# A post-norm attention and MoE kernel: three groups of routed sequences instead of seven, experts' rows cleared by an AND, the results' zeros written behind the attention, and more closing steps per matmul step

## The chip, the cores and the metric

The kernel runs on one core of one Trainium2 chip. The metric is the device time of one execution in microseconds. Before the change the median of three runs is 878.83 us (878.65 to 879.22). The profile shows one further execution of its own.

## What is computed

Input `x` has 16 sequences of 512 tokens with 128 features, all float32. Two layers follow, each with a residual and a LayerNorm behind it (post-norm). Cut to what matters here:

```python
# layer 1: linear attention, 16 heads of 8, causal, no softmax
q, k, v = silu(x @ Wq), silu(x @ Wk), x @ Wv          # q and k turned by cos/sin of position
out = ((q @ k.T) * mask) @ v @ Wo * sigmoid(x @ G1 @ G2)
x = layernorm(x + layernorm(out) * gamma + beta)
# layer 2: shared MLP plus a routed one, 8 experts, top 2, capacity 1280
logits = (x * rsqrt(mean(x * x) + eps)) @ router_w.T
topk_p, topk_i = top_k(softmax(logits), 2)            # weights: topk_p / sum(topk_p)
dispatch = argsort(~sel, stable=True)[:, :capacity]    # the first 1280 tokens of each expert
routed = scatter_add(w * valid * (silu(xg @ rg) * (xg @ ru)) @ rd)
shared = (silu(x @ sg) * (x @ su)) @ sd
x = layernorm(x + shared + routed)
```

Of an expert's 1280 places only the first `count` are taken by tokens; the others must add nothing.

## The kernel before

The attention goes by chunks of 128 tokens, 64 of them (`NT`), four to a sequence. The main loop (L799) runs over chunk times `t` and writes out by hand, engine by engine, what TensorE, ScalarE, VectorE and GpSimd do; only the order of SyncE's transfers is left to the framework, which issues them in one queue. In step `t` the loop projects chunk t + 2 (`project`, L419: the matmul at L423 is the first of its step), transposes chunk t + 1 (`turn_over`), makes the energies of chunk t (L506, masked on VectorE at L513) and the values of chunk t - 1 (L539, L548), and updates the running state (`remember`).

Into these steps four other streams are woven.

- `after(b)` (L557) is a generator of some fourteen stages. It finishes a sequence once its four chunks are done: output projection (L563), gate, two LayerNorms, the transposed copy `x1T`, and the router's logits. `advance` takes it on.
- `shared_steps` (L122) is the shared MLP, cut into 24 steps for a sequence: eight gate steps (L134, silu at L136), eight up steps (L147, multiply at L148 into `h`), and eight half down steps (L157, L162). They stand in one list, `feed`, 384 in all. `shared(t)` takes one when its sequence is ready; the loop calls it twice a chunk.
- `route(b0, b1)` (L628) is a generator that routes the tokens of a group of sequences: softmax (Exp at L654, which needs another ScalarE table than Silu and Tanh), the two best experts, then the rank of each token in its expert from two matmuls (L700, L701) and a scan, with `count` carried from group to group. It is 31 VectorE instructions over [128, n, 8] elements, n being the chunks of the group. `sprinkle` takes a few of its stages after each part of a step. `groups` (L191) has seven entries: 4, 4, 2, 2, 2, 1 and 1 sequences.
- When a group is routed, its scatters (two for each chunk, 128 in all) go into `scatters`. `scatter_behind` (L746) sends one: an indirect DMA from GpSimd (L733) that writes 128 rows of `x1` to their places in `xg_dram`. A small GpSimd instruction on `beat` ahead of it paces it to the compute. A row has 132 floats: 128 features, the token's number, the first expert and two weights.

Behind the last chunk a second loop (L847, the tail) goes on with one MLP step at a time, until `turns`, `todo` and `scatters` are empty and twelve further steps (`over`) have passed. One scatter goes out in two steps.

Two DRAM tensors need contents before they are used. `y_dram` (2 x 8192 rows) takes the experts' results and must be zero where no result comes. `xg_dram` holds the experts' rows, and a place that no token takes must read as zeros with the token number `NOBODY`, so that its result goes out of bounds and is dropped. `fill` (L410) writes both in steps 1 to 16 of the main loop: eight DMAs of 1 MB from the tile `zero` (L412), then eight of 660 KB from the tile `empty` (L414). ScalarE makes both tiles (`nought`, L278).

The second part runs the experts. `load_expert` (L879) fetches weights and rows; `turn_rows` (L892) transposes the rows in three parts of 512, 512 and 256 (L899, L900); `targets_of` (L902) works out targets and weights. For each part there are four gate and up matmuls (L1008, L1010; silu at L1012, multiply at L1013). `backs` holds the down projections (L922), each ending in an indirect DMA to `y_dram` (L928). The list `aside` makes the next expert's transposes during the second part of this one.

The final phase (L1034) takes what `feed` still has, one step at a time. Every second step it calls `add_up` (L947), which adds one of the two y rows of a sequence (L955); on every step, once the y rows are there (`landed`), it calls `an_end` (L1025), which takes one stage of `finish_lot` (L963): statistics of one tile (L102, L104), the reciprocal root (pow on GpSimd at L110; after the last silu a Sqrt on ScalarE at L116 and L118), and the scaled copy `res` (L981). A lot is four tiles, but the last four tiles are lots of one. When `feed` is empty the loop goes on with these stages alone.

Of the kernel before, what the change touches and what calls it, by code (L numbers as in the profile page):

```python
# [27 lines left out]
R = D + 4  # L28
NOBODY = 1.0e6
LN_EPS = 1e-5  # L30
# [16 lines left out]
def tile_kernel(  # L47
# [45 lines left out]
    logits = keep.tile([P, NT, E], F32, name="logits")  # L93
    idx = keep.tile([P, 2, NT], I32, name="idx")
    sg_sb = keep.tile([P, IS], F32, name="sg_sb")
    su_sb = keep.tile([P, IS], F32, name="su_sb")
# [93 lines left out]

    groups = [(0, 4), (4, 8), (8, 10), (10, 12), (12, 14), (14, 15), (15, 16)]  # L191
    with ExitStack() as ph:
# [21 lines left out]
        with tc.manual_schedule(engines=ORDERED):  # L214
# [68 lines left out]
            th_sb = cst.tile([P, D + HALF], F32, name="th_sb")  # L283
            nc.scalar.copy(th_sb, pth)
# [12 lines left out]
            cst_tok = cst.tile([P, NC, 2, 16, 2, 8], F32, name="cst_tok")  # L297
            zero = hp.tile([P, 4 * N], F32, tag="h", name="zero")
            empty = hp.tile([P, NS, R], F32, tag="h", name="empty")
            scratch = hp.tile([P, 10, D + HALF], F32, tag="h", name="scratch")  # L300
            turns_of = cst.tile([P, D + HALF], F32, name="turns_of")
            nc.vector.tensor_scalar(turns_of, pth, 1.0 / (2.0 * math.pi), None, ALU.mult)
# [31 lines left out]
        with tc.manual_schedule(engines=ORDERED):  # L334
            angles(0, pth)
            sines(0)
            angles(1, th_sb)
            same(0)

            causal = cst.tile([P, 3, HALF], F32, name="causal")
            nc.gpsimd.tensor_tensor(causal[:, 0, 0:1], scratch[:, 0, 0:1], zcol, ALU.mult)
            nc.gpsimd.memset(causal, 1.0)
            bmask = cst.tile([P, 64], F32, name="bmask")
            nc.gpsimd.memset(bmask, 1.0)
            nc.gpsimd.affine_select(
                bmask, bmask, pattern=[[-16, 8], [0, 8]], compare_op=ALU.is_ge, fill=0.0, base=0, channel_multiplier=1
            )
# [12 lines left out]
            count = cst.tile([P, E], F32, name="count")  # L362
# [4 lines left out]
            toki = cst.tile([P, NT], I32, name="toki")  # L367

        def constants_of_routing():
# [11 lines left out]
            nc.gpsimd.iota(toki, pattern=[[P, NT]], base=0, channel_multiplier=1)  # L381
            nc.vector.tensor_copy(x1[:, :, D], toki)

        def beginning(t):
# [10 lines left out]
        def beginning_done(t):  # L395
            if t == 0:

                nought(zero, 4 * N)
            elif t == 1:

                nought(empty.rearrange("p r d -> p (r d)"), NS * R)
                nc.gpsimd.memset(empty[:, :, D], NOBODY)
            elif t == 2:
                constants_of_routing()


# [221 lines left out]
        def route(b0, b1):  # L628
# [4 lines left out]
            def wide(name):  # L633
                return rp.tile([P, n, E], F32, tag=name, name=f"{name}_{b0}")
# [68 lines left out]
            nc.scalar.copy(tots[:, :, 1:], pin[:, 1].rearrange("p t e -> p e t"))  # L703
            inside = wide("inside")
            nc.scalar.copy(inside, pin[:, 0])
# [7 lines left out]
            yield  # L713
            rank = wide("rank")
            nc.vector.tensor_tensor(rank, sums[:, :, :n].rearrange("p e t -> p t e"), inside, ALU.add)
# [82 lines left out]
        with tc.manual_schedule(engines=ORDERED):  # L798
            for t in range(-2, NT + 1):  # L799
# [46 lines left out]
            t, over, waited = NT + 1, 12, 0  # L846
            while turns or todo or scatters or over:  # L847
                if not (turns or todo or scatters):
                    over -= 1
# [11 lines left out]
                if t % 2 == 0:  # L861
                    scatter_behind(latest[0])
                t += 1


    with ExitStack() as ph:
# [22 lines left out]

        xgTs, targets = {}, {}  # L890

# [10 lines left out]
        def targets_of(e):  # L902
# [89 lines left out]
        with tc.manual_schedule(engines=ORDERED):  # L992
            load_expert(0)
            load_expert(1)
            for o0, n in parts:
                turn_rows(0, o0, n)
            targets_of(0)
            backs = []
            for e in range(E):
                rg_sb, ru_sb, rd_sb, _ = got[e]  # L1000
                for o0, n in parts:
                    aside = []
                    if o0 == parts[1][0] and e + 1 < E:
                        aside = [lambda q=q: turn_rows(e + 1, *q) for q in parts] + [lambda: targets_of(e + 1)]
                    h = ep.tile([P, IR // P, N], F32, tag="eh", name=f"eh_{e}_{o0}")
# [28 lines left out]
            while feed or ends:  # L1034
# [62 lines left out]
```

## Time and profile before

| What | Value |
|---|---|
| median of the runs | 878.83 us |
| the profiled execution: time, span | 876.59 us, 874.7 us |
| granted TensorE clock, mean | 0.987 |
| ScalarE table loads | 16 of 1.283 us, 7 of them at L654 and as many behind those |
| MLP steps in the attention loop, in the tail, in the final phase (by the program's order) | 102, 124, 158 |
| scatters still to send when the attention ends | 56 of 128 |
| y_dram fills | 8 of 1024 KB, issued from 20.2 to 42.7 us |
| xg_dram fills | 8 of 660 KB, issued from 43.2 to 55.8 us |
| scatters | 128, 1039 ns of GpSimd each, from 181.6 to 494.6 us |
| experts' rows: first load issued, landed | 498.13, 502.62 us |
| last TensorE instruction ends | 860.8 us |

How to read it: an engine's busy time is the time in which one of its instructions ran; a matmul's end is modelled, so TensorE can be busy and still be slowed. A row of a timeline gives start, length, engine, line, operation, written and read tiles, how many alike were merged, and in brackets the idle time of the engine before it with what ended it; "issue" there means that nothing recorded was waited for. Float32 matmuls appear twice, as two passes. One view lists the busy time of each engine in chosen stretches of the span.

### The profile page before, as it was taken

What the parts mean: (1) busy time and instruction counts of PE and PEld (TensorE: products, weight loads), DVE (VectorE), ACT (ScalarE), POOL (GpSimd) and SP (SyncE); (2) the same over time, 40 slices, a digit from 0 to 9 for tenths busy, and PEclk for the clock granted to TensorE, in tenths of its full rate; (3) what the DMA queues carried; (4) which work ended last, traced back from release to release, by engine and by line L of the source; (5) the groups of instructions that cost most, each with busy time, mean ns of one, the idle gap of its engine ahead of it and who ended that gap; (6) DMA issues with size and microseconds to landing.
All of it is one profiled execution on the core that took longest, in us unless ns stands there. A gap on an engine that the chain in (4) does not pass through costs nothing. (4 is left out here: it accounts for less than half of the span.)

```text
span 874.7 us, 24501 instructions
## 1 busy us (share of the span) xinstructions
PE 826.3 (94%) x9792; PEld 567.3 (65%) x9792; DVE 554.1 (63%) x1705; ACT 449.4 (51%) x1302; POOL 334.2 (38%) x443
## 2 busy tenths in 40 slices
PE   6789999999989999999999999999999999999993
PEld 4566667667855765766666657777676776666663
DVE  7588888998888888978533343333333324785454
ACT  7677777577776767564322223333333332433434
POOL 2122222156655556486766413433333431001100
PEclk9899999999999999999999999999999999999997
DMA  7881111011111110000000233322132003650011
GB/s 215 323 343 34 32 34 33 30 36 58 58 40 52 57 52 27 22 29 16 11 6 1 87 88 92 95 80 65 60 92 64 25 25 112 178 169 25 25 37 48
DMA packets 64340, 62.87 MB, mean 72 GB/s; under 512 B 6180, under 2 KB 55132, under 8 KB 63202
## 3 DMA queue, kind: packets, MB, share of 16 engines
q1 hardware_dynamic: 57426, 50.35, 18.4%
q0 software_dynamic: 6656, 10.69, 3.7%
q8 instruction: 77, 1.26, 0.6%
q10 hardware_dynamic: 144, 0.26, 0.1%
q14 instruction: 37, 0.30, 0.1%
HBM read 32.62 MB, written 31.88 MB: 74 GB/s over the span
## 5 line engine op out<-in xcount | busy, mean ns | idle before, releaser
L733 POOL DMA_INDIRECT xg_dram<-x,idx x128 | 133.0, 1039 | 42.1 <-issue 36.7
L136 ACT ACTIVATE sl<-pg 128x512 f32<-128x512 f32 x128 | 76.2, 596 | 125.4 <-PE pg L134 124.6
L1013 DVE TENSOR_TENSOR eh<-esl,peu 128x512 f32<-128x512 f32 (+1 forms) x96 | 57.5, 599 | 127.8 <-PE peu L1010 127.8
L928 POOL DMA_INDIRECT y_dram<-y,to x80 | 77.8, 972 | 154.1 <-ACT y L926 154.1
L148 DVE TENSOR_TENSOR h<-sl,pu 128x512 f32<-128x512 f32 x128 | 87.5, 684 | 77.0 <-PE pu L147 64.6
L134 PE MATMUL pg<-x1T,sg_sb 128*128 128x512 f32 x256 | 131.9, 597 | 1.5 <-ACT sl L136 0.7
L147 PE MATMUL pu<-x1T,su_sb 128*128 128x512 f32 x256 | 131.0, 593 | 1.0 <-ACT sl L136 1.0
L513 DVE TENSOR_TENSOR et<-pe,causal 128x384 f32<-128x384 f32 x256 | 124.4, 547 | 9.6 <-PE pe L506 9.5
L157 PEld LDWEIGHTS pd<-sd_sb,h 128*128 128x128 f32 x1024 | 118.7, 192 | 5.8 <-issue 5.2
L157 PE MATMUL pd<-sd_sb,h 128*128 128x128 f32 x1024 | 121.9, 275 | 0.2 <-DVE add L494 0.2
L110 POOL TENSOR_TENSOR rstd<-ve,neghalf 128x4 f32<-128x4 f32 x44 | 47.2, 1073 | 194.2 <-DVE ve L108 168.0
L922 PEld LDWEIGHTS ped<-rd,eh 128*128 128x128 f32 x640 | 84.0, 192 | 24.6 <-issue 22.7
L1008 PE MATMUL peg<-xgT,rg 128*128 128x512 f32 (+1 forms) x192 | 84.6, 522 | 0.0
L1010 PE MATMUL peu<-xgT,ru 128*128 128x512 f32 (+1 forms) x192 | 84.4, 521 | 0.0
L922 PE MATMUL ped<-rd,eh 128*128 128x128 f32 x640 | 84.3, 275 | 0.0
L1012 ACT ACTIVATE esl<-peg 128x512 f32<-128x512 f32 (+1 forms) x96 | 50.5, 526 | 55.9 <-PE peg L1008 53.9
L147 PEld LDWEIGHTS pu<-x1T,su_sb 128*128 128x128 f32 x256 | 45.7, 190 | 46.0 <-issue 39.9
L926 ACT ACTIVATE y<-ped,wt 128x128 f32<-128x128 f32 x80 | 29.4, 368 | 84.6 <-PE ped L922 84.6
L134 PEld LDWEIGHTS pg<-x1T,sg_sb 128*128 128x128 f32 x256 | 44.3, 191 | 38.4 <-issue 33.7
L506 PE MATMUL pe<-q,kT 32*64 32x192 f32 x2048 | 62.1, 341 | 3.3 <-issue 2.8
L423 PE MATMUL pq<-W,xT 128*128 128x384 f32 x128 | 60.3, 554 | 4.6 <-ACT vlow L444 2.6
L448 DVE TENSOR_TENSOR hat<-qk,cst_tok 128x512 f32<-128x512 f32 x64 | 45.0, 704 | 20.4 <-ACT qk L431 20.3
(178 smaller groups left out, 1260.4 us busy)
## 6 DMA issues: line engine op xcount, KB each, us to landing
y_dram<-zero SPq DMA_DIRECT2D x8, 1024.0 KB, 11.5
y<-y_dram SPq DMA_DIRECT2D x32, 256.0 KB, 3.3
xT<-xt SPq DMA_DIRECT2D x15, 384.0 KB, 3.1
xg_dram<-empty SPq DMA_DIRECT2D x8, 660.0 KB, 9.2
xg<-xg_dram SPq DMA_DIRECT2D x8, 660.0 KB, 4.5
x<-x SPq DMA_DIRECT2D x16, 256.0 KB, 3.5
o<-res SPq DMA_DIRECT2D x15, 256.0 KB, 2.3
xg_dram<-x,idx POOLq DMA_INDIRECT x128, 2.3
```

Source lines behind the costliest of these rows:

```text
L134: nc.tensor.matmul(pg, sg_sb[:, ts(i, P)], seq, start=True, stop=True)
L136: nc.scalar.activation(sl, pg, AF.Silu)
L147: nc.tensor.matmul(pu, su_sb[:, ts(i, P)], seq, start=True, stop=True)
L148: nc.vector.tensor_tensor(h[i // half][:, i % half, :], h.pop(("s", i)), pu, ALU.mult)
L157: nc.tensor.matmul(pd, h[k][:, i - k * half, ts(c, P)], sd_sb[:, i, :], start=(i == 0), stop=(i == IS // P - 1))
L506: nc.tensor.matmul(pes[g][mine, s], kT[rows, s, mine], q2[rows, s, 3 * i : 3 * i + 3], start=(s == 0), stop=(s == 1),)
L513: nc.vector.tensor_tensor(et.rearrange("p s k n -> p s (k n)"), pes[g].rearrange("p s k n -> p s (k n)"), causal.rearrange("p k n -> p (k ...
L733: i = nc.gpsimd.indirect_dma_start(out=xg_dram[:, :], out_offset=bass.IndirectOffsetOnAxis(ap=idx[:, k, t : t + 1], axis=0), in_=x1[:, t, ...
L922: nc.tensor.matmul(pd, h[:, i, ts(c, P)], got[e][2][:, i, :], start=(i == 0), stop=(i == IR // P - 1))
L928: i = nc.gpsimd.indirect_dma_start(out=y_dram[:, :], out_offset=bass.IndirectOffsetOnAxis(ap=to[:, at : at + 1], axis=0), in_=y, in_offset ...
L1008: nc.tensor.matmul(pg[:, :n], rg_sb[:, ts(i, P)], xgTs[e][:, ds(o0, n)], start=True, stop=True)
L1010: nc.tensor.matmul(pu[:, :n], ru_sb[:, ts(i, P)], xgTs[e][:, ds(o0, n)], start=True, stop=True)
```

## The change

Five things are changed.

- `groups` becomes (0, 6), (6, 12), (12, 16). The last one is routed behind the attention.
- `xg_dram` is no longer filled. `clear_rows` makes two masks for each expert from the place's number and `count`: all ones where the place is taken, else 0; and `NOBODY`, now the integer 1 << 20, where it is not. The rows are ANDed with the first as integers, and the targets ORed with the second.
- `y_dram` is zeroed in the tail: sixteen DMAs of 512 KB, one every fourth step, from the first 512 floats of a tile of the attention (`vpads[0][0]`), which ScalarE clears when the attention is over. The tail also waits for `fills`.
- `aside` is kept over the parts of an expert, since it now has seven entries instead of four.
- In the final phase `an_end` is called twice on every odd step, and twice on every step once `feed` is empty.

Some small tiles move: `count` and `slotno` are kept to the end, `th_sb`, `turns_of`, `inside` and `rank` share the space of others.

```diff
-NOBODY = 1.0e6
+NOBODY = 1 << 20
...
-    groups = [(0, 4), (4, 8), (8, 10), (10, 12), (12, 14), (14, 15), (15, 16)]
+    groups = [(0, 6), (6, 12), (12, 16)]
...
+            nc.gpsimd.iota(sloti, pattern=[[P, NS]], base=0, channel_multiplier=1)
+            nc.vector.tensor_copy(slotno, sloti)
...
         def beginning_done(t):
-            if t == 0:
-
-                nought(zero, 4 * N)
-            elif t == 1:
-
-                nought(empty.rearrange("p r d -> p (r d)"), NS * R)
-                nc.gpsimd.memset(empty[:, :, D], NOBODY)
-            elif t == 2:
+            if t == 2:
                 constants_of_routing()
...
-        y_rows = y_dram.rearrange("(p q r) d -> p q (r d)", p=P, r=4 * N // D)
-        x_rows = xg_dram.rearrange("(p q r) d -> p q (r d)", p=P, r=NS)
+        y_rows = y_dram.rearrange("(p q r s) d -> q p r (s d)", p=P, r=2, s=N // D)

         def fill(i):
-            if i < 8:
-                nc.sync.dma_start(y_rows[:, i, :], zero)
-            elif i < 16:
-                nc.sync.dma_start(x_rows[:, i - 8, :], empty.rearrange("p r d -> p (r d)"))
-
+            nc.sync.dma_start(y_rows[i], zero.unsqueeze(1).to_broadcast([P, 2, N]))
+
+        fills = list(range(2 * T * D // (P * 2 * N)))
...
-                if 1 <= t < 17:
-                    fill(t - 1)
...
             t, over, waited = NT + 1, 12, 0
-            while turns or todo or scatters or over:
-                if not (turns or todo or scatters):
+
+            zero = vpads[0][0].rearrange("p a b d -> p (a b d)")[:, 0:N]
+            nought(zero, N)
+            while turns or todo or scatters or fills or over:
+                if not (turns or todo or scatters or fills):
                     over -= 1
...
                     scatter_behind(latest[0])
+                if t % 4 == 1 and fills:
+                    fill(fills.pop(0))
                 t += 1
...
+        def clear_rows(e, o0, n):
+
+            if o0 == 0:
+                taken[e] = ok = ep.tile([P, 2, NS], I32, tag="ok", name=f"ok_{e}")
+                nc.vector.tensor_scalar(ok[:, 0], slotno, count[:, e : e + 1], -1.0, ALU.is_lt, ALU.mult)
+                nc.vector.tensor_scalar(ok[:, 1], slotno, count[:, e : e + 1], float(NOBODY), ALU.is_ge, ALU.mult)
+            here = slice(o0 // P, (o0 + n) // P)
+            rows = got[e][3][:, here, :].bitcast(I32)
+            nc.vector.tensor_tensor(
+                rows, rows, taken[e][:, 0, here].unsqueeze(2).to_broadcast([P, n // P, R]), ALU.bitwise_and
+            )
...
             nc.vector.scalar_tensor_tensor(to, second, float(T), xg[:, :, D], ALU.mult, ALU.add)
+            nc.vector.tensor_tensor(to, to, taken[e][:, 1], ALU.bitwise_or)
...
             for o0, n in parts:
+                clear_rows(0, o0, n)
+            for o0, n in parts:
                 turn_rows(0, o0, n)
             targets_of(0)
-            backs = []
+            backs, aside = [], []
...
                 for o0, n in parts:
-                    aside = []
                     if o0 == parts[1][0] and e + 1 < E:
-                        aside = [lambda q=q: turn_rows(e + 1, *q) for q in parts] + [lambda: targets_of(e + 1)]
+                        for step in (clear_rows, turn_rows):
+                            aside += [lambda q=q, f=step, e=e: f(e + 1, *q) for q in parts]
+                        aside.append(lambda e=e: targets_of(e + 1))
...
                 an_end()
+                if begun % 2 == 1 or not feed:
+                    an_end()
```

By the changed program's order the attention loop has 102 MLP steps as before, the tail 156 and the final phase 126.

More of the change, by code (lines that the diff above doesn't have):

```diff
@@ L94, in tile_kernel @@
     idx = keep.tile([P, 2, NT], I32, name="idx")
+    count = keep.tile([P, E], F32, name="count")
+    slotno = keep.tile([P, NS], F32, name="slotno")
     sg_sb = keep.tile([P, IS], F32, name="sg_sb")
@@ L282, in tile_kernel @@
             nc.tensor.matmul(pth, ones[0:1, :], th_row, start=True, stop=True)
-            th_sb = cst.tile([P, D + HALF], F32, name="th_sb")
+            th_sb = wk1.tile([P, D + HALF], F32, tag="w", name="th_sb")
             nc.scalar.copy(th_sb, pth)
@@ L297, in tile_kernel @@
             cst_tok = cst.tile([P, NC, 2, 16, 2, 8], F32, name="cst_tok")
-            zero = hp.tile([P, 4 * N], F32, tag="h", name="zero")
-            empty = hp.tile([P, NS, R], F32, tag="h", name="empty")
             scratch = hp.tile([P, 10, D + HALF], F32, tag="h", name="scratch")
-            turns_of = cst.tile([P, D + HALF], F32, name="turns_of")
+            turns_of = wk1.tile([P, D + HALF], F32, tag="o", name="turns_of")
             nc.vector.tensor_scalar(turns_of, pth, 1.0 / (2.0 * math.pi), None, ALU.mult)
@@ L361, in tile_kernel @@
             startrow = cst.tile([P, E], F32, name="startrow")
-            count = cst.tile([P, E], F32, name="count")
             goes_on = {}
@@ L367, in tile_kernel @@
             toki = cst.tile([P, NT], I32, name="toki")
+            sloti = cst.tile([P, NS], I32, name="sloti")
         def constants_of_routing():
@@ L703, in route @@
             nc.scalar.copy(tots[:, :, 1:], pin[:, 1].rearrange("p t e -> p e t"))
-            inside = wide("inside")
+            inside = rp.tile([P, n, E], F32, tag="sel", name=f"inside_{b0}")
             nc.scalar.copy(inside, pin[:, 0])
@@ L713, in route @@
             yield
-            rank = wide("rank")
+            rank = rp.tile([P, n, E], F32, tag="prob", name=f"rank_{b0}")
             nc.vector.tensor_tensor(rank, sums[:, :, :n].rearrange("p e t -> p t e"), inside, ALU.add)
@@ L888, in load_expert @@
             got[e] = rg_sb, ru_sb, rd_sb, xg
-        xgTs, targets = {}, {}
+        xgTs, targets, taken = {}, {}, {}
+        def clear_rows(e, o0, n):
[8 more added lines that the diff above has]
+            )
         def turn_rows(e, o0, n):
```

## The prediction, made before the changed kernel was run

> **What bounds the kernel now.** I read the page first, then the busy times by stage, then TensorE's timeline inside the stages that lose time, then what stands behind its last matmul.
>
> ```profile
> span 874.7 us, 24501 instructions
> PE 826.3 (94%) x9792; PEld 567.3 (65%) x9792; DVE 554.1 (63%) x1705; ACT 449.4 (51%) x1302; POOL 334.2 (38%) x443
> ...
> DMA  7881111011111110000000233322132003650011
> ```
>
> TensorE is the bound, so only its idle time and stretched stages can be won. The windows name the stages: start, first chunks, one calm group of four, attention with the shared MLP, tail, experts, final phase, and what follows the last matmul. Columns: busy us (instructions) of PE, PEld, DVE, ACT, POOL, then granted clock, DMA share, GB/s.
>
> ```profile
> 0.00:23.15 23.15, 14.49 (x192) 9.38 (x192) 17.07 (x63) 17.19 (x60) 6.07 (x26) 0.91 0.74 226
> 23.15:66.02 42.87, 34.62 (x868) 26.15 (x869) 29.63 (x87) 29.17 (x107) 8.94 (x19) 0.93 0.84 328
> 66.02:84.93 18.91, 17.44 (x448) 12.94 (x446) 17.88 (x59) 14.48 (x54) 6.05 (x7) 1.00 0.13 39
> 84.93:392.00 307.07, 293.98 (x6014) 208.25 (x6013) 267.26 (x878) 215.56 (x721) 151.73 (x183) 0.99 0.13 40
> 392.00:503.80 111.80, 110.11 (x520) 68.61 (x518) 54.28 (x184) 34.13 (x62) 71.55 (x117) 1.00 0.10 26
> 503.80:729.00 225.20, 223.88 (x1118) 155.90 (x1119) 79.47 (x164) 81.75 (x179) 77.75 (x80) 1.00 0.23 66
> 729.00:860.80 131.80, 131.80 (x639) 86.10 (x637) 81.81 (x239) 50.60 (x103) 12.12 (x12) 1.00 0.31 90
> 860.80:874.70 13.90, 0.00 (x0) 0.00 (x0) 6.73 (x37) 6.56 (x18) 0.00 (x0) 0.68 0.19 57
> ```
>
> PE idles 8.7, 8.3, 1.5, 13.1, 1.7, 1.3, 0 and 13.9 us in them. The second stage is the one with the fills (8.4 MB of zeros and 5.4 MB of empty rows, DMA share 0.84); the last is pure tail. TensorE's timeline in the second:
>
> ```profile
> 35.89 0.29 PE L548 MATMUL pout<-et,vpad 128*32 128x64 f32 x7
> 39.27 0.55 PE L548 MATMUL pout<-et,vpad 128*32 128x64 f32 x25 [3.09 <-issue]
> ```
>
> Seven of 32 alike matmuls run, PE stands 3.09 us waiting for nothing recorded, and the other 25 follow. The same cut is at 30.82 (1.35), 56.04 (2.21) and 63.40 (0.58), with the DMA engines 83 to 100% busy at each. I read it as instructions that come late behind the fills.
>
> **The first fills go (L414 for good, L412 to the tail).** Eight chunks from 23.15 to 66.02 take 42.87 us; the four calm ones after them take 18.91. If all eight cost what the calm ones do, 42.87 - 2 x 18.91 = 5.1 is won. But the first four carry hardly any steps of `after`, and a chunk without them takes 3.4 (45.85 to 49.21, 66.02 to 69.50): 3 x 3.4 + 4.7 + 18.91 = 33.8, or 9.1 won. I take 8.0, near the upper end, because the cuts, and the 0.6 to 0.8 clock behind them, lie in those first four. It includes ACT's 1.30 for `empty`. ACT's 1.90 for `zero` wins nothing: ACT waits for DVE right behind it (sines at 21.16). The added iota and copy for `slotno` are two instructions of 0.2, hidden on POOL and 0.2 on DVE.
>
> Here a rule speaks against me. The Trainium skill (Runtime: NRT & Kernel Launch, Instruction fetch mechanics) says that fetching is hidden, since the sequencer issues more slowly than the buffer fills. By it the cuts are something else and stay: the start would win ACT's 1.30 alone. The row shows cuts only while the fills run (none over 0.3 us without a named releaser later, in six thousand matmuls of attention), so I go by the row.
>
> **Three groups instead of seven.** A step of attention starts with L423. Without routing four chunks take 22.50 us (184.66 to 207.16), by chunk 5.41, 5.31, 6.58, 5.20. With it:
>
> ```profile
> 335.76 0.91 PE L423 MATMUL pq<-W,xT 128*128 128x384 f32 x2
> 341.07 0.91 PE L423 MATMUL pq<-W,xT 128*128 128x384 f32 x2
> 351.25 0.81 PE L423 MATMUL pq<-W,xT 128*128 128x384 f32 x2
> ```
>
> The chunk at 341.07 takes 10.18 instead of 6.58. Summed over the six chunks of each route against the calm ones: (0,4) 38.54 - 34.39 = 4.2; (4,8) 40.87 - 34.39 = 6.5; (8,10) 38.41 - 34.39 = 4.0; (10,12) 6.1, its last chunk estimated from (4,8)'s. Sum 20.8. The cheap two lie beside down steps (L157), the dear two beside up steps, which also load ACT and DVE. By the changed program's order, (0,6) routes in chunks 34 to 39, four of them with up steps, and (6,12) exactly where (10,12) did. So 6.5 and 6.1, plus wider rows: the 31 DVE instructions of a route take 8.5 us for two sequences and 8.8 and 10.3 for four, about 1.1 more per two sequences; 20.8 of stretch against 36.0 of DVE time makes 0.6 of that count: 0.6 for (0,6), 1.2 for (6,12). After: 14.4. Won 6.4 (4.7 if the width counts in full, 10.7 if both get the cheap place).
>
> The table loads are inside this: each route costs two of
>
> ```profile
> 340.36 1.28 ACT L654 ACT_TABLE_LOAD   x1
> ```
>
> and the copy before it ends at 340.35. The Trainium skill (ScalarE: Activation LUTs, What ACT_TABLE_LOAD costs) adds a drain of 1.38 us to each switch. By it four loads fewer would free 10.6 us of ACT; the row has no such idle, so 5.1.
>
> In the tail three routes become one; PE's gaps from them (390.49, 399.46, 400.36, 415.32: 0.96 + 0.27 + 0.42 + 0.69 = 2.3) shrink by two thirds: 1.5 (0 to 2.3).
>
> **The zeros in the tail.** Sixteen DMAs of 512 KB, one in four steps. On SP they stand before the first expert's loads only. 1 MB took 2.44 us between landings in the start, so 1.2 us in every 3.5: a third of the DMA engines, which have a share of 0.10 there. Scatters need 1.38 us of POOL per 1.75. PE runs 520 matmuls in 112 us here against 868 in 43 us, so late instructions should not return. ACT's 512 zeros, about 0.6, fall between silus. Cost 0. The tail itself gets 32 steps longer (124 to 156 by the order, since 72 scatters instead of 56 are left when attention ends), and the final phase loses the same 32 (158 to 126): TensorE does them in either place, 0.
>
> **The AND.** Per expert 528 + 528 + 264 elements on DVE. The nearest row with a broadcast operand is L448, 704 ns for 512; so 0.7 + 0.7 + 0.4 and three small ones, 2.3 us in an expert of 27.2 us in which DVE works about 9.5. Behind each stands one `eh` multiply, with three PSUM buffers in front of PE: 0. Only expert 0 is exposed: its rows landed at 502.62, PE's feed ended at 503.79, and it stood 0.93 + 0.40. In the new order DVE holds the three ANDs ahead of the last two `h` multiplies, and the first transpose waits for the rows: landing + 1.8 to 3.2 instead of + 2.1. I take +1.0 (0 to 3).
>
> **Denser last steps.** From the first to the last y add the DVE order of before has 33 adds, 21 `h`, 24 pairs of statistics, 10 `pd` adds, 11 small ones; start to start these take 0.60, 0.60, 0.41, 0.21, 0.15: 46.0 us beside 54.0 of PE. After: 32, 22, 34, 9, 16, so 50.6; and in three lots `nb` follows `ve` at once and DVE waits out POOL's pow (1.07): 53.9. That is as much as PE has. Three PSUM buffers smooth it; I take +1.5 (0 to 4).
>
> What is won stands behind the last matmul:
>
> ```profile
> 860.84 0.29 DVE L162 TENSOR_TENSOR x1T<-pd,x 128x128 f32<-128x128 f32 x1 [1.49 <-PE pd L157]
> ...
> 867.76 0.16 DVE L118 RECIPROCAL rstd<-root 128x1 f32<-128x1 f32 x1 [1.53 <-ACT root L116]
> ...
> 871.65 0.49 ACT L981 ACTIVATE res<-x1T,nb,rstd 128x128 f32<-128x128 f32 x1 [0.47 <-ACT root L116]
> ```
>
> Two lots of four and four single tiles follow it. In the new order only tile 60's reciprocal and three more tiles do: from 867.76 to 872.14 that is 4.4, after the add's 0.3, and 2.6 to the span's end: 7.3 instead of 13.9. Won 6.6 (5.5 to 7.2).
>
> **Sum.** -8.0 - 6.4 - 1.5 + 1.0 + 1.5 - 6.6 = -20.0. The profiled execution took 876.59 (span 874.7), so 856.6 for such a one; the median of the runs is 2.24 above it: 878.83 - 20.0 = 858.8.
>
> **Rivals.** (a) Forecast, 0.68. (b) The cuts of the start are not the fills' doing: the start wins 1.3, the sum is -13.3, 865.5. For it: no record names a DMA. Against: where they lie. 0.13. (c) DVE bounds the final phase: adds and 1.5 statistics steps per step fit only just; if each of the about eight lots in that stretch costs PE 0.7, +5.5 instead of +1.5: 862.8. 0.14. (d) Slower: the AND runs at a price no row of its kind shows. L661, a multiply with a broadcast operand, once took 1.83 us for 64 elements, 28 ns each, beside POOL's work; at that price an expert's AND takes 37.7 us, DVE 47, against 27.2 of PE: +160 in all. The AND costs time from 13.4 ns an element on (17.7 us free / 1320) and makes the kernel slower from about 15.3. Against: L448, L513 and L1013 all take about 1.4. 0.03. The last 0.02 is for no gain that can be told.
>
> Best ends together give -29, worst -8; with (b) and (c) 851 to 867. A measurement of this kernel can tell about 0.2% (1.8 us) from no change. Faster 0.94, same 0.02, slower 0.04.
>
> **What would show it.** The stage from t = 4 to t = 12 at 33 to 38 us, with no "issue" cut; three Exp loads; chunks 34 to 39 and 58 to 63 stretched by about 7 each; DVE over 90% while the y adds run; about 7 us behind the last matmul. I am wrong if the cuts remain without fills, if they appear in the tail, or if PE shows gaps in the final phase.

## The result, and the profile after

| | before | after |
|---|---|---|
| median of the runs | 878.95 us (878.65 to 879.22, 4 runs) | 866.40 us (865.53 to 869.30, 4 runs) |
| the profiled execution: time, span | 876.59, 874.7 us | 865.53, 863.8 us |
| last TensorE instruction ends | 860.8 us | 856.7 us |

The ratio is 0.9863, with a 95% interval of 0.984 to 0.9887: 1.4% faster. I had said 858.8. The range (851 to 867) holds the median by 0.6 us, and one of the four runs (869.30) lies outside it; 7.5 of the 20 us that I forecast did not come.

The page of the kernel after, in the lines that answer to those of before:

```profile
span 863.8 us, 24377 instructions
PE 825.7 (96%) x9776; PEld 568.8 (66%) x9776; DVE 554.2 (64%) x1629; ACT 433.0 (50%) x1279; POOL 337.2 (39%) x451
...
DMA  6011111110111110048000032231122200365211
```

TensorE's busy time is the same to 0.6 us (826.3, 825.7), so the gain is idle time of TensorE, as expected. The first quarter of the DMA row is now almost empty, and the zeros show as the 4 and 8 behind the attention. A second view, busy time by stage of the kernel after (PE, PEld, DVE, ACT, POOL, clock, DMA share, GB/s), with start, chunks 4 to 11, the calm four, attention, tail, experts, final phase and what follows the last matmul:

```profile
23.83:59.40 35.57, 33.93 (x869) 25.45 (x869) 31.93 (x90) 27.96 (x106) 9.32 (x18) 0.95 0.11 33
59.40:78.39 18.99, 17.52 (x446) 13.04 (x446) 16.61 (x55) 14.45 (x54) 5.58 (x6) 1.00 0.13 39
...
717.00:856.70 139.70, 133.96 (x659) 90.22 (x657) 82.83 (x256) 56.50 (x123) 25.13 (x25) 0.99 0.32 94
856.70:863.80 7.10, 0.00 (x0) 0.00 (x0) 2.65 (x15) 2.56 (x7) 0.00 (x0) 0.77 0.18 51
```

The second stage went from 42.87 to 35.57 us with the same 868 or so matmuls; the last from 13.9 to 7.1. In the final phase, where PE had no idle time before, 5.7 us of it has come.

For the account I cut the span at instructions that both kernels have: the first matmul of chunks 4, 12, 16, 17 and 63, the first transpose of expert 0, the start of the last down projection of expert 7, and PE's end. 32 of the MLP steps moved from the final phase to the tail: 12 gate and 12 up steps of 0.86 each and 8 half down steps of 0.89, 27.8 us. The column "without them" takes these 27.8 out of both.

| Stretch | before | after | difference | without them | predicted |
|---|---|---|---|---|---|
| start to chunk 4 | 23.15 | 23.83 | +0.68 | +0.68 | 0 |
| chunks 4 to 11 | 42.87 | 35.57 | -7.30 | -7.30 | -8.0 |
| chunk 16 | 5.29 | 6.97 | +1.68 | +1.68 | 0 |
| the rest of chunks 12 to 62 | 297.48 | 291.83 | -5.65 | -5.65 | -6.4 |
| chunk 63, tail, to expert 0 | 135.93 | 162.23 | +26.30 | -1.5 | -1.5 + 1.0 |
| experts | 220.81 | 220.78 | -0.03 | -0.03 | 0 |
| final phase to PE's end | 135.28 | 115.47 | -19.81 | +8.0 | +1.5 |
| behind PE's end | 13.87 | 7.14 | -6.73 | -6.73 | -6.6 |

The last but one column comes to -10.9, the one beside it to -20.0. Of the 9.1 between, 6.5 lie in one row: the final phase.

What happened there is read from the timeline of all engines in the kernel after. First come a lot's variance `ve` on VectorE, its pow on POOL (`rstd`) and the VectorE instruction that uses the result (`nb`), then VectorE's queue up to the add that frees a down buffer (one of the two PSUM buffers, `ps_d`, that take the down results):

```profile
807.76 0.16 DVE L110 TENSOR_SCALAR ve<-mv 128x4 f32<-128x4 f32 x1
808.09 1.01 POOL L112 TENSOR_TENSOR rstd<-ve,neghalf 128x4 f32<-128x4 f32 x1 [6.81 <-DVE ve L110]
809.13 0.16 DVE L986 SCALAR_TENSOR_TENSOR nb<-mv,rstd 128x4 f32<-128x4 f32 x1 [1.21 <-POOL rstd L112]
809.21 0.69 DVE L150 TENSOR_TENSOR h<-sl,pu 128x512 f32<-128x512 f32 x1
...
812.64 0.18 DVE L106 BATCH_NORM_AGGREGATE mv<-st 128x2 f32<-128x6 f32 x1
812.74 0.26 DVE L164 TENSOR_TENSOR x1T<-pd,x 128x128 f32<-128x128 f32 x1
812.92 0.68 DVE L963 TENSOR_TENSOR x<-x,y 128x512 f32<-128x512 f32 x1
813.05 3.55 PEld L159 LDWEIGHTS pd<-sd_sb,h 128*128 128x128 f32 x18 [3.11 <-DVE x1T L164]
813.05 3.63 PE L159 MATMUL pd<-sd_sb,h 128*128 128x128 f32 x17 [2.92 <-DVE x1T L164]
```

VectorE stands still for 1.21 us. `ve` is issued in an even step, and `nb` two calls of `an_end` later, which are both in the next step. That step is a gate step, which gives VectorE nothing to do, so `nb` stands right behind `ve` in its queue. Everything behind it is late: two `h`, y adds, two pairs of statistics, and only then the down add at 812.74. TensorE has filled both down buffers by then and stands for 2.92 us. Two more such stops begin at 765.04 (1.69) and 787.88 (1.11); ahead of them VectorE waited 1.12 and 1.21 us for pow. The other 2.3 of the 8.0 are matmuls that run longer: PE is busy 109.75 us for work that takes 107.50 where nothing waits (the first experiment). Some 1.6 of these go with the longest stop: around its end the granted clock fell to 0.50 for 3.4 us, in which PE was busy for 3.11.

```profile
812.74:816.16 3.42, 3.11 (x14) 3.11 (x15) 2.12 (x10) 0.14 (x1) 1.01 (x1) 0.50 0.17 50
```

### The profile page after: what moved, and what is told of

Same layout as the page of the kernel before. It is cut to its first block, busy times and chain, and to the rows that moved or that the text cites. A ratio compares the mean times of both kernels' runs of the same rounds, so it can differ in the third digit from the quotient of the medians.

```text
span 863.8 us, 24377 instructions
## 1 busy us (share of the span) xinstructions
PE 825.7 (96%) x9776; PEld 568.8 (66%) x9776; DVE 554.2 (64%) x1629; ACT 433.0 (50%) x1279; POOL 337.2 (39%) x451
## 5 line engine op out<-in xcount | busy, mean ns | idle before, releaser
L159 PE MATMUL pd<-sd_sb,h 128*128 128x128 f32 x1024 | 125.1, 279 | 5.9 <-DVE x1T L164 5.7
L159 PEld LDWEIGHTS pd<-sd_sb,h 128*128 128x128 f32 x1024 | 121.3, 195 | 12.1 <-DVE x1T L164 6.3
L112 POOL TENSOR_TENSOR rstd<-ve,neghalf 128x4 f32<-128x4 f32 x46 | 49.5, 1076 | 195.1 <-DVE ve L110 188.8
L1021 PEld LDWEIGHTS peu<-xgT,ru 128*128 128x128 f32 x192 | 36.5, 190 | 32.2 <-issue 28.9
```

What stands on the lines that cost most here:

```text
L159: nc.tensor.matmul(pd, h[k][:, i - k * half, ts(c, P)], sd_sb[:, i, :], start=(i == 0), stop=(i == IS // P - 1))
L1021: nc.tensor.matmul(pu[:, :n], ru_sb[:, ts(i, P)], xgTs[e][:, ds(o0, n)], start=True, stop=True)
```

## The experiments

There are eleven experiments, and the kernel before ran again beside them: it took 879.23 us (median of 9) beside the first four below, 885.06 (of 7) beside `zeros_early`, `zeros_burst`, `groups_alone` and `apart_over14`, and 879.25 (of 7) beside `apart_psum`, `burst_long` and `seven_groups`. So a ratio is always to the kernel before that ran beside it. Stages are read from one trace of each kernel. How far that carries is seen where kernels do not differ: the final phase of the changed kernel took 115.47 to 115.70 us in four of them, but chunks 12 to 62 took 298.8 to 301.6 in eight.

### The final phase: one closing step, pow set apart, later, more buffers

A closing step is one call of `an_end`.

**One closing step per matmul step (`single_end`).** The whole edit:

```diff
                 an_end()
-                if begun % 2 == 1 or not feed:
-                    an_end()
```

> Theory A (in the final phase VectorE is full: y adds, 1.5 closing stages per step and waits for GpSimd's pow): with one closing stage per step TensorE shows no gap waiting for L164 and its last matmul ends about 8 us earlier than in the changed kernel (849 instead of 857), but 23 pairs of statistics stand behind it instead of 3, some five lots of 2.4 us more, so about 870 in all. Theory B (the y loads come late): the gaps stay, and the time is 878.

Measured: 871.39 us (870.09 to 874.60, 6 runs), ratio 0.9925 (0.9903 to 0.9947). Its final phase and what follows it:

```profile
740.34:847.84 107.50, 107.50 (x531) 70.95 (x529) 68.11 (x195) 40.32 (x82) 10.67 (x11) 1.00 0.36 105
847.84:868.40 20.56, 0.00 (x0) 0.00 (x0) 11.79 (x65) 12.11 (x33) 0.00 (x0) 0.62 0.27 77
```

TensorE is busy without a break, and the final phase takes just what is due (135.28 - 27.8 = 107.5). So the 8.0 us are wholly the denser closing steps' doing. They buy 20.5 - 7.1 = 13.4 behind the last matmul. The 13.4 is more than the 6.6 that I counted: in this version 23 pairs of statistics are left behind the last down result, since 32 steps fewer stand in the final phase.

**Pow set apart (`pow_apart`).** Two empty stages after the pow instead of one, and a call of `an_end` that meets one goes on to another lot. So `nb` comes three calls after `ve` instead of two, and the two calls between do work of other lots, where an empty stage cost a call before:

```diff
             if not roots:
-                yield True
+                yield "idle"
+                yield "idle"
...
-                    if went is not False:
+                    if went is not False and went != "idle":
                         return
```

> Two turns of other lots are put between the variance (ve) and the use of its root (nb), so that VectorE never waits out GpSimd's pow. Theory A with the pow waits as the larger part: five lots of 1.1 us each, 4 to 6 us faster than the changed kernel, 861. Theory A with the mere amount of VectorE work: within 1 us. Theory B: no change.

Measured: 858.72 us (858.12 to 862.27, 4 runs), ratio 0.9783 (0.975 to 0.9815). The same lot in the timeline of this run:

```profile
807.05 0.17 DVE L110 TENSOR_SCALAR ve<-mv 128x4 f32<-128x4 f32 x1
...
807.40 1.01 POOL L112 TENSOR_TENSOR rstd<-ve,neghalf 128x4 f32<-128x4 f32 x1 [5.65 <-DVE ve L110]
...
809.16 0.13 DVE L987 SCALAR_TENSOR_TENSOR nb<-mv,rstd 128x4 f32<-128x4 f32 x1
809.21 0.28 DVE L164 TENSOR_TENSOR x1T<-pd,x 128x128 f32<-128x128 f32 x1
...
809.55 3.73 PE L159 MATMUL pd<-sd_sb,h 128*128 128x128 f32 x31 [0.47 <-DVE x1T L164]
```

The pow costs what it cost, but VectorE works on meanwhile: `nb` waits for nothing, here and in every other lot, and TensorE's stop is 0.47 instead of 2.92. The other two are 0.79 and 0.80. The final phase took 110.38 instead of 115.47: 5.1 of the 8.0 went with the waits for pow, the low clock at the longest stop among them. The rest, 2.9, I put down to VectorE's own work in crowded steps. Besides, since no call is spent on an empty stage, two lots of single tiles end earlier, and 4.84 us are left behind the last matmul instead of 7.14.

**Later (`late_dense`).** The second call only once no y adds are left, but then on every step, not on odd ones alone:

```diff
-                if begun % 2 == 1 or not feed:
+                if not adds or not feed:
                     an_end()
```

> One closing stage per step while y rows are still added, two afterwards. Theory A: VectorE is 85% busy in the adds, as before the change, and the 8 us come back: 858 to 860. Theory B: gaps at the same places in the adds, 865.

Measured: 867.27 us (864.49 to 869.81, 4 runs), ratio 0.9857 (0.9822 to 0.9891): no better than the changed kernel, and my expectation failed. No stop is left while the adds run, but the stops come later, in TensorE's timeline:

```profile
834.20 5.46 PE L159 MATMUL pd<-sd_sb,h 128*128 128x128 f32 x32 [2.07 <-DVE x1T L164]
852.89 3.28 PE L159 MATMUL pd<-sd_sb,h 128*128 128x128 f32 x27 [1.36 <-DVE h L150]
```

The final phase took 113.08, 2.4 less than after, but 9.4 us stand behind the last matmul, 2.2 more. It isn't the y adds alone that make the stops. Ahead of the first VectorE waited 1.21 us for pow, with `nb` right behind `ve` again. Ahead of the second it waited 0.61 for pow and then 1.43 for a silu, which stood behind two copies to `res` in ScalarE's queue.

**More down buffers (`psum_four`).** What TensorE can do ahead over VectorE's delays:

```diff
-name="ps_g", bufs=3
+name="ps_g", bufs=2
...
-name="ps_d", bufs=2
+name="ps_d", bufs=4
```

> Four PSUM buffers for the down results and two each for gate and up, instead of two and three. Theory C (TensorE stops only because two down buffers are too few while VectorE lags for a short time): 6 to 8 us faster, 859. Theory A (VectorE is full on average): about 2 us faster at most, or slower where gate and up lack a buffer.

Measured: 862.56 us (861.68 to 863.05, 4 runs), ratio 0.9815 (0.9791 to 0.984). The final phase took 112.34, 3.1 less than after, though VectorE still waits for pow as before. TensorE's waits at the down steps are gone; three shorter ones stand at the gate steps, which now have two buffers:

```profile
779.69 1.12 PE L136 MATMUL pg<-x1T,sg_sb 128*128 128x512 f32 x2 [0.57 <-ACT sl L138]
794.74 1.13 PE L136 MATMUL pg<-x1T,sg_sb 128*128 128x512 f32 x2 [0.77 <-ACT sl L138]
801.46 1.12 PE L136 MATMUL pg<-x1T,sg_sb 128*128 128x512 f32 x2 [0.66 <-ACT sl L138]
```

**Both (`apart_psum`).** The edits of `pow_apart` and `psum_four` together.

> The changed kernel with both repairs: two empty stages between the call of GpSimd's pow and the instructions that use it, and four PSUM buffers for the half down steps (one gate buffer fewer, two instead of three). Pow apart alone took 858.7 and left 2.9 us in the final phase (110.4 where 107.5 is due). Theory R: those 2.9 us are VectorE's work of single steps (two stages of statistics, an add, a down add in one step), and two more down buffers let TensorE run ahead over it: final phase 108 to 109, 856 to 857.5. Rival: with two gate buffers the gate steps wait for the silu instead (gaps of 0.6 to 0.8 at L136 stood in the run with four down buffers), and what one buffer gives the other takes: 858.5 to 860.

Measured: 856.15 us (855.09 to 860.15, 4 runs), ratio 0.9744 (0.9722 to 0.9766). The final phase took 108.78, with one stop of 0.56 left at a gate step, and 4.84 stood behind it: theory R. It is the best version of the study, 23.1 us under the kernel before that ran beside it. Against `pow_apart` the intervals of the ratios overlap (0.9783 and 0.9744), so the total does not tell them apart; their final phases, of one trace each, do (110.38 and 108.78). The two repairs overlap: 5.1 and 3.1 us alone, 6.7 together.

**Pow apart, a longer tail (`apart_over14`).** The edits of `pow_apart`, and fourteen further steps instead of twelve:

```diff
-            t, over, waited = NT + 1, 12, 0
+            t, over, waited = NT + 1, 14, 0
```

> pow_apart with fourteen covering steps instead of twelve before the first expert. If TensorE only lacked work while the first rows come (2.6 us idle), about 1.7 us of it is covered: 857. If VectorE's AND, queued ahead of the last multiplies, is what holds it, the gap moves and the time stays at 858.7.

Measured: 864.15 us (861.59 to 866.13, 4 runs), ratio 0.976 (0.9731 to 0.9789). The intervals overlap with those of `pow_apart`, so this is inconclusive. In its trace the stop at expert 0's first transpose shrank from 2.54 to 0.90, but 1.37 came at an up step ahead of it, which waited for an `h` that stood behind an AND: the exposed part of the head only changed places.

### The zeros: in the start, in short bursts, in a long one

**Zeros in the start (`zeros_early`).** The sixteen fills go to chunks 1 to 8, two in each, from a tile that is there anyway, and ScalarE makes no zeros for them (this and the next two kernels leave the zeros out, and write other data of the same size):

```diff
-            nc.sync.dma_start(y_rows[i], zero.unsqueeze(1).to_broadcast([P, 2, N]))
+            nc.sync.dma_start(y_rows[i], W.unsqueeze(1).to_broadcast([P, 2, N]))
...
+                if 1 <= t < 9:
+                    fill(fills.pop(0))
+                    fill(fills.pop(0))
                 shared(t)
```

> The changed kernel with the sixteen 512 KB transfers to y_dram put back into chunks 1 to 8 (their source is the weights W, so that they write W in place of zeros and the output is not the reference's; ScalarE's clearing is left out). Theory F (transfers that keep the DMA engines full hold back TensorE's instructions): cuts named issue come back in the start and the eight chunks from t = 4 take 38 to 41 us instead of 35.6. Theory G (fetching is hidden; the empty rows or ScalarE's clearing made the difference): 35.6 and no cut.

Measured once: 877.98 us. Chunks 4 to 11 took 39.58 us, against 35.40 to 37.62 in the ten kernels with no fills there. One cut is back, in TensorE's timeline, and a clock of 0.50 for 3.41 us behind it:

```profile
35.63 0.29 PE L540 MATMUL pout<-et,vpad 128*32 128x64 f32 x7
37.91 0.91 PE L540 MATMUL pout<-et,vpad 128*32 128x64 f32 x25 [1.99 <-issue]
```

It falls behind the seventh of 32 alike matmuls, as before the change. The changed kernel runs through that place:

```profile
35.17 0.41 PE L531 MATMUL pout<-et,vlow 128*32 128x64 f32 x16
35.40 0.63 PE L540 MATMUL pout<-et,vpad 128*32 128x64 f32 x32
```

A cut at the same instruction in two kernels speaks for a border between two pieces of the instruction stream, and the trace's transfers say so too. Those of kind "instruction", 16 KB each, in the order of time (us):

```
before       17.6  29.8  37.0  40.4  49.0  55.9  61.6    cuts of PE end at 32.2, 39.3, 58.3
after        19.5  26.7  32.1  36.2  40.7  45.7  50.9    no cut
zeros_early  21.4  29.5  35.6  39.0  44.7  49.7  54.8    a cut ends at 37.9
```

The fourth cut of the kernel before ends at 64.0. All five end 2.3 to 2.4 us after such a transfer begins, and so do the two of `groups_alone` below, which keeps the old fills. In the start of the ten kernels without fills there is no cut at all. After the change the transfers come every 4 to 7 us, and PE never waits for one. That the cuts are late instructions is read from these times; no record ties a stop to a transfer.

**Two short bursts (`zeros_burst`).** Eight fills each in chunks 24 and 34 of the attention, from finished parts of `x1T` instead of `W`:

```diff
+                if t in (24, 34):
+                    for _ in range(8):
+                        fill(fills.pop(0))
                 shared(t)
```

> The changed kernel with the same sixteen transfers sent in two bursts of eight in the middle of the attention, when x1T of sequences 3 and 5 is ready (they write rows of x1T in place of zeros, so the output is not the reference's). Each burst keeps the DMA engines full for about 10 us, in which TensorE goes through some 200 pairs of weight load and matmul. Theory F: one or two cuts of 1 to 3 us named issue inside the bursts, the attention 2 to 5 us longer. Theory G: none, unchanged. If xT of the next sequence comes late behind a burst, the gap stands before L415 instead.

Measured once: 874.35 us. No cut followed; one "issue" of 0.43 is all. The 16 engines had a share of 0.94 for 10 us, and one 16 KB transfer came some 3 us late. The expected cuts missed, and my reading of them as something that full DMA engines do anywhere fell with that, unless the bursts were too short. Hence the next one.

**One long burst (`burst_long`).** All sixteen fills twice, 16.8 MB, in chunk 24, from a finished part of `x1T`:

```diff
+                if t == 24:
+                    for i in fills + fills:
+                        fill(i)
+                    fills.clear()
                 shared(t)
```

> The changed kernel, but the fills go out in one burst in chunk 24 of the attention, all sixteen twice over, 16.8 MB, from a finished part of x1T, with no zeros made for them (what they write isn't zero, which this kernel leaves out). At the start's 330 GB/s they hold the 16 DMA engines full for 45 to 50 us, as long as the start of the kernel before did; the two short bursts of 4.2 MB held them for 10 us and gave no cut. Theory L: it is the length that counts. TensorE's instructions are fetched by the same engines, some way ahead, and only a lasting queue uses that lead up: from some 10 to 20 us after the burst's begin TensorE stops at least twice for 1 to 3 us with no releaser recorded, 3 to 7 us in all, in a stretch where the changed kernel has none. Theory S: the cuts belong to the start (what is loaded or run there for the first time), not to full DMA engines: none here, and the attention takes what the changed kernel's takes, within 1 us.

Measured once: 873.68 us. The stretch of the burst, by engines:

```profile
127.00:171.00 44.00, 43.90 (x952) 33.26 (x954) 35.85 (x116) 30.53 (x111) 11.04 (x12) 1.00 1.01 369
```

The DMA engines are full for 44 us, and TensorE is busy for 43.9 of them. Chunks 25 to 30 take 33.8 us, and 33.4 in the changed kernel. Theory L is out. The burst costs in another way: an ordinary load stands behind it in SP's queue.

```profile
171.32 0.66 PE L602 MATMUL px<-ident,x 128*128 128x128 f32 x4
175.72 1.49 PE L415 MATMUL pq<-W,xT 128*128 128x384 f32 x2 [3.75 <-DMA xT<-xt]
```

Chunk 31 takes 10.38 instead of 6.47, and chunk 32, at a granted clock of 0.75, 6.96 instead of 5.20. So full DMA engines alone don't cut TensorE; fills in the start do. What in the start makes the difference stays open. The distance between two transfers of instructions doesn't tell: it was 6.1 us ahead of the one that ended the cut of `zeros_early`, and 8.9 at the beginning of the long burst, with no cut.

### The groups: alone, and undone

**Three groups on the kernel before (`groups_alone`).** `inside` and `rank` share space as in the change; else only:

```diff
-    groups = [(0, 4), (4, 8), (8, 10), (10, 12), (12, 14), (14, 15), (15, 16)]
+    groups = [(0, 6), (6, 12), (12, 16)]
```

> The kernel before with the three groups alone (and the shared space for inside and rank). Attention from t = 12 on about 6 us shorter, the tail 32 steps longer and the final phase as much shorter, its last matmul some 9 us earlier than before; but one closing stage per step leaves 23 pairs of statistics behind it instead of 12, 20 us instead of 14. About 876, 3 us faster than before.

Measured once: 884.58 us, beside 885.06 for the kernel before: 0.5 instead of the 3 expected, and nothing that can be told. The final phase lost the 27.8 us to the tail, but 20.5 us stand behind the last matmul instead of 13.9, as in `single_end`: with fewer matmul steps in the final phase, one closing step for each leaves 23 pairs of statistics over. So the shorter final phase gives back 6.6 us. The win in the attention is not shown here: chunks 12 to 62 took 303.58 us, where the trace of the kernel before has 302.77, and the last matmul ended at 862.35 instead of 860.80, not some 9 us earlier. But that trace is from other runs of the kernel before, of 879 us and not 885, and none was kept from the runs beside this one. The start kept cuts (2.38 and 2.50), since it kept its fills.

**Seven groups in the kernel after (`seven_groups`).** The same edit, undone in the changed kernel.

> The changed kernel with the seven groups of before: the routing alone undone. By the program's order the MLP steps are 102, 124 and 158 again, as before. Theory G: a route costs what its place in the attention costs, as I summed from the chunks, so the stretch from chunk 12 to chunk 63 takes 304 to 305.5 us instead of 298.8, the tail's routes 3 us more; the 32 steps moved cost nothing in either place; the final phase keeps its waits for pow (135.3 due for 158 steps, 142 to 144 expected): 874 to 876. Rival: the groups alone gave 0.5 us on the kernel before, so their number hardly matters: the stretch stays within 2 us of 298.8, and 866 to 869.

Measured: 870.52 us (869.45 to 871.79, 4 runs), ratio 0.9908 (0.9886 to 0.993). Chunks 12 to 62 took 304.77 us, within theory G's 304 to 305.5, against 298.80 with three groups: 6.0. In `apart_psum`, whose runs stood beside these, it is 298.76; with chunk 16 left out of both (6.97 and 5.29, see below) the difference is 4.3. From there to expert 0 it took 137.99, which is 3.5 more than the changed kernel's once the 27.8 are taken out. Both stages are as theory G has them; the total is 4 us below it, since the final phase lost 6.4 to its waits, not 7 to 9, and 4.83 us stood behind the last matmul instead of 7.14. So the routes cost about what their places cost. In the total it shows barely: the interval of this ratio begins at 0.9886, and that of the changed kernel ends at 0.9887.

## Why the prediction was right in kind and too low by 7.6 us

The range held because it had been drawn wide enough for the two likeliest rivals, (b) and (c). The steps came out as follows.

**The start, -8.0: measured -7.30.** The cuts are gone, and chunks without steps of `after` take 3.36 and 3.59. The step that put the cuts down to the fills held: they are in the three kernels with fills in the start and in none of the ten without. (The low clock that I saw behind the cuts stood behind one of them only: 0.50 from 39.69 to 43.10.) The wider reading, instructions late wherever the DMA engines are full, did not hold. The rule of the Trainium skill that fetching is hidden (Runtime: NRT & Kernel Launch, Instruction fetch mechanics), by which the start would win 1.30, does not account for the 7.30 here; it agrees with the attention, where 44 us of full engines passed without a cut.

**The routes in the attention, -6.4: measured -5.65,** and 4.3 to 6.0 from the other side (`seven_groups`). TensorE's projections around the second route, in the kernel after:

```profile
328.58 0.91 PE L415 MATMUL pq<-W,xT 128*128 128x384 f32 x2
338.98 0.81 PE L415 MATMUL pq<-W,xT 128*128 128x384 f32 x2
344.18 0.91 PE L415 MATMUL pq<-W,xT 128*128 128x384 f32 x2
```

10.40, with six sequences in the route, where the two-sequence route of before took 10.18 in the same place. The first route stretches its six chunks by 41.16 - 34.39 = 6.8, the second its five up to chunk 62 by 35.11 - 27.82 = 7.3; predicted were 7.1 and 7.3. There are three Exp loads, as forecast:

```profile
L646 ACT ACT_TABLE_LOAD x3 | 3.8, 1283 | 0.1
```

**The tail's route, -1.5: about -3.1,** which is what the row's -1.5 leaves when the AND's +1.6 (below) is taken out, and 3.5 in `seven_groups`. I had counted only TensorE's recorded gaps; what the rest is made of stays open.

**The zeros in the tail, 0: measured 0, but not as I had them.** I expected one fill in 3.5 us, a third of the DMA engines. SP issued all sixteen between 379.6 and 398.2, one in 1.2 us, and the engines were full for 20 us. By stretches of 10 us, in the kernel after:

```profile
380.00:390.00 10.00, 9.96 (x35) 4.47 (x35) 8.25 (x26) 4.60 (x10) 9.15 (x13) 1.00 0.98 350
390.00:400.00 10.00, 10.00 (x82) 8.72 (x81) 3.69 (x19) 3.10 (x7) 8.71 (x14) 1.00 1.02 358
```

TensorE stood for 0.04 us in them. So the step was right, but not for the lower load. My other reason, the few matmuls of the tail, this stretch leaves open; `burst_long` shows that it isn't needed, with 952 matmuls in 44 us of full engines.

**The AND, 0 in the experts and +1.0 at their head: measured -0.03 and +1.6.** VectorE's groups by form, in the kernel after:

```profile
L895 DVE TENSOR_TENSOR xg<-xg,ok 128x528 int32<-128x528 int32 x16 | 11.1, 702 | 2.2 <-DMA xg<-xg_dram 2.2
L895 DVE TENSOR_TENSOR xg<-xg,ok 128x264 int32<-128x264 int32 x8 | 3.4, 425 | 0.0
```

702 and 425 ns, where 0.7 and 0.4 were taken from L448's row; the slow rival's 28 ns an element did not come. At the head the three ANDs stand among VectorE's last two `h`, and the first transpose came 2.54 + 0.35 us after TensorE's feed instead of 0.93 + 0.40; in `groups_alone`, without the AND, the first of these gaps is 0.93.

**Denser last steps, +1.5: measured +8.0.** This is the step that failed, a term mis-sized by 6.5, and here one of my own signs of being wrong came: gaps of TensorE in the final phase (2.92, 1.69 and 1.11). The prediction had found the three lots in which VectorE waits for pow and added their waits to its work: 53.9, as much as TensorE has. That sum came out: 49.96 us of work and 3.5 of waits. Then it said that three PSUM buffers smooth it. Two things in this were wrong. The down steps have two buffers, not three (`ps_d`); with four, 3.1 came back. And a sum over 54 us says nothing about a single wait. VectorE was busy for 49.96 of the 61.7 us of the y adds, 81%, where I had said over 90%. Before the change it was 45.90 of 55.50, 83%, and TensorE lost nothing. What counts is what stands behind the stopped instruction in VectorE's queue. 1.2 us of waiting grew to 2.92 on TensorE, because two `h`, two y adds and two pairs of statistics were queued ahead of the one add that frees a buffer. Setting pow apart gave 5.1 back. The rival of a VectorE bound (c) had the right place and sign, and its +5.5 was nearer, but its mechanism was the smaller part: at most the 2.9 that were left.

**Behind the last matmul, -6.6: measured -6.73.** VectorE's timeline there (the first line is the last add):

```profile
856.72 0.29 DVE L164 TENSOR_TENSOR x1T<-pd,x 128x128 f32<-128x128 f32 x1 [1.08 <-PE pd L159]
856.93 0.15 DVE L120 RECIPROCAL rstd<-root 128x1 f32<-128x1 f32 x1
...
860.80 0.49 ACT L989 ACTIVATE res<-x1T,nb,rstd 128x128 f32<-128x128 f32 x1 [0.47 <-ACT root L118]
```

One reciprocal and three tiles, as counted from the order.

**What no step had: +1.68 in chunk 16, +0.68 in the start.** In chunk 16 the same instructions ran at a lower clock (columns as above):

```profile
75.47:78.88 3.41, 1.94 (x41) 1.20 (x30) 2.82 (x7) 3.08 (x10) 1.77 (x3) 1.00 0.02 5
78.88:82.29 3.41, 3.41 (x10) 1.97 (x9) 0.69 (x1) 1.91 (x8) 0.00 (x0) 0.50 0.00 0
82.29:85.70 3.41, 3.41 (x101) 2.13 (x100) 2.21 (x11) 2.26 (x8) 0.21 (x1) 1.00 0.00 0
```

The clock was 0.50 for 3.41 us, which is 1.7 us of lost work, behind a wait of 1.41 us at 76.03. The change does not decide this. All 13 traces have this wait. Ten have the low clock behind it, and chunk 16 takes 6.76 to 6.98; `before`, `apart_psum` and `apart_over14` do not have it, and chunk 16 takes 5.29. In every trace the granted clock changes only at whole multiples of 3.41 us from its other changes, so time is divided into windows of that length. In the ten traces the wait began 0.05 to 1.25 us after a window's begin, in the three 1.66 to 1.95 us. So whether 1.7 us are lost goes with where the wait falls in the windows, and that differs from trace to trace. (It is not the whole rule: of eleven like waits some 19 us earlier ten fit it, and one, which began 0.03 us after a window's begin, was followed by no low clock.) The +1.68 is bad luck of the profiled execution. The 0.68 also comes and goes from run to run of like kernels (23.15 in `seven_groups`, 24.58 in `apart_psum`); I explain nothing by it.

Finally, the forecast started from the medians, where the profiled execution of before lies 2.4 us under its median and that of after 0.9. By the profiled ones the gain is 11.1, by the medians 12.5.

## What to carry to other kernels

When a cheap step asks another engine for a small result, don't issue the use of it right behind the request on an in-order queue: put other work between them. Price such a wait by what is queued behind it and by the buffers of the engine that waits for that, not by the busy share of the queue; here an engine at 81% stopped its neighbour for 2.92 us. And a change that moves matmul steps out of a phase takes away the cover of whatever was issued one per step, so the two belong in one sum.

## What the hardware showed beyond this

- Full DMA engines did not slow TensorE by themselves: 44 us at 369 GB/s cost it 0.1 us of idle time and 0.4 us over six chunks. What did cost was order in one queue: a load behind 16.8 MB of fills held TensorE for 3.75 us.
- In the start, TensorE stopped behind fills with nothing recorded that it waited for: 1.35, 3.09, 2.21 and 0.58 us before the change, 2.38 and 2.50 with the same fills in `groups_alone`, and 1.99 with 8.4 MB instead of 13.8. Each stop ended 2.3 to 2.4 us after the start of a 16 KB transfer of instructions.
- A short stop of TensorE is paid twice at times: behind a wait of 1.41 us the clock was 0.50 for 3.41 us (chunk 16: 6.97 instead of 5.29), and so it was behind one of 3.75 us (chunk 32 of `burst_long`: 6.96 instead of 5.20). Behind the shorter wait it goes with the place of the wait in windows of 3.41 us, so two single traces of like kernels can differ by 1.7 us in a stage for no cause of the kernel's own.
